# A Mamba block with an FP4 feed-forward: state carries, norm statistics and evictions go to ScalarE, the residual add to the feed-forward's head

## The chip, the cores and the metric

One core of a Trainium2 chip runs the whole program. The metric is the device time of one execution in microseconds (us), the median of the runs shown. The engines are TensorE (PE; its weight loads are shown as PEld), VectorE (DVE), ScalarE (ACT), GpSimd (POOL) and SyncE (SP), which issues all DMAs of this kernel. Each engine runs its instructions in the order in which they were written; semaphores make one wait for another.

## The reference

The input x has 8192 rows of 512 numbers. A layernorm with a scale and a shift from a modulation vector, a Mamba mixer, a gated residual, a second layernorm, a feed-forward with FP4-quantized operands, and a second gated residual:

```python
h = _layernorm(x) * (1 + ca) + sa
x = x + ga * mamba(h)
h = _layernorm(x) * (1 + cb) + sb
x = x + gb * ffn(h)

# mamba(h): 1024 inner channels (DI), 16 states (NS), delta rank 32
xc, z = split(h @ W_in.T)
xc = silu(causal_conv4(xc))                 # 4 taps, per channel
dlt, B, C = split(xc @ W_xproj.T)
delta = softplus(dlt @ W_dt.T + b_dt)
s = exp(delta * A) * s + delta * B * xc     # a scan over the 8192 rows
y = sum_n(s * C) + xc * D
out = (y * silu(z)) @ W_out.T
# ffn(h): silu(q(h) @ q(w_gate).T) * (q(h) @ q(w_up).T), quantized again, @ q(w_down).T
```

Everything is computed in fp32.

## The kernel before, in words

**Three stages.** A prologue (about 155 us) quantizes the gate and up weights and prepares the first chunk. The scan part runs to about 4310 us. The feed-forward part takes the rest, 64 tiles of 128 rows.

**The scan part** cuts the 8192 rows into 16 chunks `k` of 512 rows (T). In a chunk the 1024 channels are 8 blocks `d` of 128 partitions, worked through in four pairs `h`; the 16 states in 8 groups `g` of two. One *slot* is one channel block with two states: 64 slots a chunk, 1024 in all, in the order k, h, g, i (i is the block within the pair). `unit(slot)` is the heart of it:

- two scans on VectorE (L454), each over 512 rows of one state: `da` (exp of delta times A, made by ScalarE into PSUM, L434) times the running state plus `db` (delta times x times B, made by GpSimd two slots ahead, L425, three buffers);
- the carry: the last column of the two scans is copied into `state`, where the same block finds it 64 slots later;
- the product with C, and its transposes into the accumulator `y` in PSUM on TensorE (`add_up`, L368).

There are two kinds of slots. A *far* slot (odd i, and g % 4 not 3: 24 of the 64) scans into an SBUF tile `hp`; its carry is a ScalarE copy (L462) and its product is made by GpSimd (L471). A *near* slot (40 of the 64) scans into the one PSUM tile `hs`; its carry is a VectorE copy (L474) and its product `hc` is made by VectorE (L476). ScalarE's order within a slot is: the first exp of the next slot, the carry (far slots), the second exp of the next slot, then the slot's side work. The PSUM holds two `da` tiles, so an exp waits until the scan of the same number one slot earlier is through.

**The side work** is put into slots by hand: `at(slot, moment, fn, ...)` files a function for a slot, and `run` calls it. The moments are BEGIN (before the scans are issued), GAP (after the scans and exps, before the next `db` and the product) and END (after the product). A table of offsets in the loop over `k` (from `for k in range(NC)` on) says which step goes where. The steps that the change touches:

- `norm`, `norm_x`, `norm_t`, `norm_out`: the layernorm of the next chunk's rows. Statistics on VectorE (bn_stats, L217 to L221), the power -1/2 on GpSimd (L223), the offset on VectorE (L230), the normalized rows on ScalarE (L232), transposes on TensorE, scale and shift on ScalarE (L247).
- `conv_mm`, `conv_raw`, `conv_diag`, `conv_taps`, `conv_act`, `conv_out`: the four-tap convolution as matmuls. `raw` holds three columns from the chunk before (`tail`) and 512 new ones. GpSimd copies the three columns in (L274) and the new tail out (L276); the second copy reads what ScalarE wrote into `raw` (L275). `conv_diag` makes the four diagonal tap matrices on ScalarE (L268).
- `prep_mm`, `prep`: delta with a softplus on ScalarE, with a table load before and after it (L327, L434). `make_du`: delta times x on GpSimd (L334), one for each block of the pair.
- `z_mm`, `z_act`, `z_out`: the z half of in_proj, its tanh on ScalarE (L353) and the silu on VectorE (L357).
- `skip_act`, `skip`: x times D into `y`. `gate` (L379): y times silu(z) on VectorE, two halves, after the pair's last slot. `gate_t`, `gate_out` (L390): transposes back.
- `out_mm`, `out_add`: out_proj, and the residual add on VectorE (L403): the rows of x are loaded again (`load_x` with key "r"), the product is added from PSUM, and the sum is stored to the DRAM tiles `x1`.

PSUM is full: one bank (`mm`) serves z, out_proj, gate_t, x_proj and half of prep_mm in turn; another (`cv`) serves the convolution, the norm's transposes and the other half.

**The feed-forward part** is put in order by a scheduler, not by hand. For each tile of 128 rows, `normed` loads the rows from `x1`, takes the layernorm (`_layernorm`, bn_stats on VectorE and the power on GpSimd), applies scale and shift on GpSimd (L808, L809) and quantizes; `up` and `down` are the matmuls with the quantization between them. `head` prepares a tile ahead.

## Time and profile before

| | us |
|---|---|
| median of 3 runs (6424.08 to 6426.37) | 6424.61 |
| profiled execution | 6427.96 |
| its span, first to last instruction | 6426.2 |
| prologue | about 155 |
| scan part, to the last scan | about 155 to 4304 |
| feed-forward part, one tile in its steady state | 31.4 |

| engine | busy us | share |
|---|---|---|
| PE | 5533.2 | 86% |
| DVE | 5079.5 | 79% |
| POOL | 4033.9 | 63% |
| ACT | 2858.3 | 44% |

The shares are means over stages with different limits, so they are read stage by stage. In the groups by line, a row gives line, engine, operation, output and inputs with their shapes, the number of instructions, their busy time in us and the mean ns of one, and then the idle time of the engine just before them with what ended it. In the timeline, a row gives start and duration in us and, in brackets, the idle time before it and who ended it. Neighbouring instructions of an engine can overlap by about 0.1 us, so what an instruction costs is read from the starts.

### The profile page before, as it was taken

The numbers are of one execution on the slowest core, as the hardware profiler recorded it, in microseconds if no ns is written. First come the engines' busy times: TensorE is split into PE (matmuls) and PEld (weight loads), VectorE is DVE, ScalarE is ACT, GpSimd is POOL, SyncE is SP. The second block draws the span as 40 slices with busy tenths as digits, with TensorE's granted clock in tenths as the row PEclk, the third lists the DMA queues.
The fourth block names the chain that finished last, engine by engine and source line by source line (L and its number), as shares of the span: only waits on it lengthen the run. The fifth ranks groups of instructions, "written<-read, shape, count | busy, mean of one in ns | idle before, by whom it ended". The sixth has DMA issues, their size and how long they took to land.

```text
span 6426.2 us, 60794 instructions
## 1 busy us (share of the span) xinstructions
PE 5533.2 (86%) x20772; PEld 3284.8 (51%) x20772; DVE 5079.5 (79%) x5711; ACT 2858.3 (44%) x4940; POOL 4033.9 (63%) x2222
## 2 busy tenths in 40 slices
PE   7788878888888888887888888767999999999999
PEld 4455555555555555555555555543444444444444
DVE  7988888888888888888888888988566666666564
ACT  5555555555555555555555555532222222222222
POOL 5888888888888888888888888872222222222221
PEclk9899888889888898988988889778999999999999
DMA  5444444444444444444444444440000000000000
GB/s 186 135 145 139 138 140 140 144 140 144 143 136 140 143 142 144 136 145 135 143 141 142 144 140 140 152 162 23 22 17 17 17 17 17 18 18 17 17 17 12
DMA packets 220557, 659.83 MB, mean 103 GB/s; under 512 B 24371, under 2 KB 36787, under 8 KB 220246
## 3 DMA queue, kind: packets, MB, share of 16 engines
q1 hardware_dynamic: 220246, 655.94, 31.4%
q8 instruction: 163, 2.67, 0.2%
q14 instruction: 148, 1.21, 0.1%
HBM read 615.48 MB, written 40.38 MB: 102 GB/s over the span
## 4 chain that ended last, share of the span: by engine, by line
PE 53%; DVE 30%; POOL 6%; ACT 5%; issue 5%; DMA 1%; DVEq 0%; SPq 0%; POOLq 0%; ACTq 0%
DVE hs L454 13%; PE pg L874 9%; PE po L891 9%; PE pu L874 9%; DVE hp L454 7%; PE po L396 6%; PE y L368 6%; DVE hc L476 5%; PE cv L254 5%; PE cv L282 4%; POOL db L425 4%; PE pz L344 2%; POOL hp L471 2%; PE pt L842 1%; DVE z L379 1%
## 5 line engine op out<-in xcount | busy, mean ns | idle before, releaser
L425 POOL TENSOR_TENSOR db<-bc,du 128x1024 f32<-128x1024 f32 x1024 | 2396.0, 2358 | 17.4 <-DVE hs L454 13.2
L434 ACT ACTIVATE da<-delta,na 128x512 f32<-128x512 f32 x2048 | 1394.3, 686 | 1548.5 <-DVE hs L454 969.5
L454 DVE TENSOR_TENSOR_SCAN hs<-da,state,db 128x512 f32<-128x512 f32 x1280 | 1647.4, 1287 | 230.6 <-POOL db L425 122.1
L368 PE MATMUL y<-ident,hc 128*128 128x128 f32 x5120 | 783.4, 303 | 457.5 <-DVE hc L476 456.9
L87 POOL TENSOR_TENSOR hq<-xn,sc 128x1408 f32<-128x1408 f32 x64 | 189.1, 2955 | 1466.3 <-DVE xn L82 1466.3
L471 POOL TENSOR_TENSOR hp<-hp,bc 128x1024 f32<-128x1024 f32 x384 | 905.4, 2358 | 186.1 <-ACT state L462 184.9
L454 DVE TENSOR_TENSOR_SCAN hp<-da,state,db 128x512 f32<-128x512 f32 x768 | 941.6, 1268 | 60.8 <-ACT da L434 54.6
L368 PEld LDWEIGHTS y<-ident,hc 128*128 128x128 f32 x5120 | 652.0, 156 | 656.4 <-DVE hc L476 570.7
L476 DVE TENSOR_TENSOR hc<-hs,bc 128x1024 f32<-128x1024 f32 x640 | 779.9, 1219 | 0.3 <-issue 0.3
L874 PE MATMUL pg<-wg,xqT 128*128 128x512 f32 (+1 forms) x1536 | 651.8, 568 | 44.0 <-ACT xqT L866 44.0
L254 PE MATMUL cv<-hT,w_in 128*128 128x512 f32 x1024 | 560.4, 698 | 128.5 <-ACT delta L327 103.3
L874 PE MATMUL pu<-wu,xqT 128*128 128x512 f32 (+1 forms) x1536 | 635.9, 557 | 0.0
L891 PE MATMUL po<-wd,hqT 128*128 128x512 f32 x1408 | 616.2, 593 | 0.0
L880 DVE TENSOR_TENSOR h<-g,pu 128x512 f32<-128x512 f32 (+1 forms) x192 | 122.9, 640 | 541.9 <-PE pu L874 528.4
L879 ACT ACTIVATE g<-pg 128x512 f32<-128x512 f32 (+1 forms) x192 | 107.7, 561 | 957.7 <-PE pg L874 957.7
L282 PE MATMUL cv<-raw,taps 128*128 128x512 f32 x1024 | 510.7, 645 | 5.9 <-POOL raw L274 4.9
L344 PE MATMUL pz<-w_in,hT 128*128 128x256 f32 x2048 | 490.7, 395 | 1.4 <-DVE z L357 1.4
L874 PEld LDWEIGHTS pg<-wg,xqT 128*128 128x128 f32 x1536 | 290.1, 192 | 361.2 <-issue 250.3
L396 PE MATMUL po<-w_o,xc 128*128 128x512 f32 x1024 | 466.7, 599 | 3.3 <-DVE xr L403 2.5
L874 PEld LDWEIGHTS pu<-wu,xqT 128*128 128x128 f32 x1536 | 291.8, 190 | 312.7 <-issue 243.5
L368 PE MATMUL y<-ident,hp 128*128 128x128 f32 x3072 | 436.5, 289 | 0.0
L368 PEld LDWEIGHTS y<-ident,hp 128*128 128x128 f32 x3072 | 389.8, 151 | 88.0 <-issue 72.4
(112 smaller groups left out, 6274.0 us busy)
## 6 DMA issues: line engine op xcount, KB each, us to landing
bc<-bc SPq DMA_DIRECT2D x1024, 512.0 KB, 4.7
xn<-in_x_dram SPq DMA_DIRECT2D x64, 256.0 KB, 4.8
xr<-in_x_dram SPq DMA_DIRECT2D x64, 256.0 KB, 4.9
x<-xr SPq DMA_DIRECT2D x64, 256.0 KB, 2.1
x<-x SPq DMA_DIRECT2D x64, 256.0 KB, 2.6
out_dram<-x SPq DMA_DIRECT2D x64, 256.0 KB, 2.0
w_in<-in_w_inT_dram SPq DMA_DIRECT2D x2, 2048.0 KB, 10.1
wm<-in_wmod_dram SPq DMA_DIRECT2D x8, 512.0 KB, 4.8
```

The costliest lines, as they stand in the source:

```text
L254: nc.tensor.matmul(ps, lhsT=w_in[:, f, o : o + P], rhs=hT[k][:, f, :], start=(f == 0), stop=(f == NK - 1),)
L282: nc.tensor.matmul(v, lhsT=taps[:, i, :], rhs=raw[:, i : i + T], start=(i == 0), stop=(i == 3))
L344: nc.tensor.matmul(pz[:, b, :], lhsT=hT[k][:, f, t0 : t0 + P], rhs=w_in[:, f, o : o + DH * P], start=(b == 0 and f == 0), stop=(f == NK - ...
L368: nc.tensor.matmul(y[:, j, i * P : (i + 1) * P], lhsT=src[:, j * P : (j + 1) * P], rhs=ident, start=start and j % 2 == 0, stop=stop, is_tr ...
L396: nc.tensor.matmul(pend["po", k, j], lhsT=xcs[k, d][:, j * P : (j + 1) * P], rhs=w_o[:, d, :], start=(d == 0), stop=(d == ND - 1),)
L425: nc.gpsimd.tensor_tensor(db, bct[slot // DH, 0], dus[k, h, i].unsqueeze(1).to_broadcast([P, GN, T]), ALU.mult)
L434: nc.scalar.activation(da, deltas[k, h][:, i, :], AF.Exp, scale=na[:, d, n : n + 1])
L454: nc.vector.tensor_tensor_scan(to[:, q, :], pend.pop(("da", slot, q)), db[:, q, :], state[:, d, n : n + 1], ALU.mult, ALU.add,)
L471: nc.gpsimd.tensor_tensor(to, to, c_rows, ALU.mult)
L476: nc.vector.tensor_tensor(hc, hs, c_rows, ALU.mult)
L874: nc.tensor.matmul(ps[:, :w], lhsT=qT[:, k, :], rhs=wt[:, k, o : o + w], start=(k == 0), stop=(k == NK - 1),)
L891: nc.tensor.matmul(po, lhsT=hT[:, f, :], rhs=wd[:, f, :], start=(f == 0), stop=(f == NF - 1))
```

## The change

State carry: all slots copy the carry on ScalarE; the VectorE copy of near slots is gone.

Norm: the statistics are taken on ScalarE. `norm_sum` copies the rows onto themselves with a running sum and scales the sum to the negative mean; `norm_var`, a slot later, squares the centred rows with a running sum and adds eps; `norm_rstd` is the power on GpSimd, at the next slot's BEGIN; `norm_x` makes the offset and the normalized rows on ScalarE.

Row tails: ScalarE copies the three columns into `raw`, and the new tail from PSUM.

out_proj: `out_keep` copies the product from PSUM into an SBUF tile on ScalarE, at GAP where `out_add` was at END, and stores it to the DRAM tiles `mo`. x isn't loaded a second time here. The feed-forward's head loads both `mo` and x and adds them on GpSimd.

Moved steps: the gate's two halves from GAP and END of the first slot after the pair to its END and the next slot's GAP; `gate_t`, `gate_out`, `skip_act` and `skip` one slot later; the first product's transposes of a pair one slot later; the second block's delta-x product to the slot before the pair begins; some of z's and out_proj's slots by one.

```diff
-        def norm(k, j):
+        def norm_sum(k, j):
             xt = xts["n", k, j]
-            st = small.tile([P, 6], F32, tag="st", name="st")
-            nc.vector.bn_stats(st, xt)
-            mv = small.tile([P, 2], F32, tag="mv", name="mv")
-            nc.vector.bn_aggr(mv, st)
+            su = small.tile([P, 1], F32, tag="su", name="su")
+            nc.scalar.activation(xt, xt, AF.Copy, accum_out=su)
+            nm = small.tile([P, 1], F32, tag="nm", name="nm")
+            nc.scalar.activation(nm, su, AF.Copy, scale=-1.0 / DM)
+            pend["nm", k, j] = nm
+
+        def norm_var(k, j):
+            xt, nm = xts["n", k, j], pend["nm", k, j]
+            xh = s1.tile([P, DM], F32, tag="xh", name=f"xh_{k}_{j}")
+            ss = small.tile([P, 1], F32, tag="ss", name="ss")
+            nc.scalar.activation(xh, xt, AF.Square, bias=nm, accum_out=ss)
             ve = small.tile([P, 1], F32, tag="ve", name="ve")
-            nc.vector.tensor_scalar(ve, mv[:, 1:2], EPS, None, ALU.add)
+            nc.scalar.activation(ve, ss, AF.Identity, bias=eps, scale=1.0 / DM)
...
+        def norm_rstd(k, j):
             rstd = small.tile([P, 1], F32, tag="rstd", name="rstd")
-            nc.gpsimd.tensor_tensor(rstd, ve, mhalf, ALU.pow)
+            nc.gpsimd.tensor_tensor(rstd, pend.pop(("ve", k, j)), mhalf, ALU.pow)
...
         def norm_x(k, j):
             off = small.tile([P, 1], F32, tag="off", name="off")
-            nc.vector.tensor_scalar(off, mv[:, 0:1], rstd, -1.0, ALU.mult, ALU.mult)
-            nc.scalar.activation(xh, xt, AF.Identity, bias=off, scale=rstd)
+            nc.scalar.activation(off, nm, AF.Copy, scale=rstd)
+            nc.scalar.activation(
+                pend["xh", k, j], xts.pop(("n", k, j)), AF.Identity, bias=off, scale=rstd
+            )
...
         def conv_raw(k, d):
-            nc.gpsimd.tensor_copy(raw[:, 0:3], tail[:, d, :])
             nc.scalar.activation(raw[:, 3 : T + 3], v, AF.Copy)
-            nc.gpsimd.tensor_copy(tail[:, d, :], raw[:, T : T + 3])
+            nc.scalar.activation(raw[:, 0:3], tail[:, d, :], AF.Copy)
+            nc.scalar.activation(tail[:, d, :], v[:, T - 3 : T], AF.Copy)
...
-        def out_add(k, j):
-            xt = xts.pop(("r", k, j))
-            nc.vector.tensor_tensor(xt, xt, pend.pop(("po", k, j)), ALU.add)
-            nc.sync.dma_start(x1[k][j * P : (j + 1) * P, :], xt)
+        def out_keep(k, j):
+            po = xp.tile([P, DM], F32, tag="x", name=f"po_{k}_{j}")
+            nc.scalar.activation(po, pend.pop(("po", k, j)), AF.Copy)
+            nc.sync.dma_start(mo[k][j * P : (j + 1) * P, :], po)
...
             carry = state[:, d, g * GN : (g + 1) * GN]
-            if far:
-                nc.scalar.activation(carry, to[:, :, T - 1], AF.Copy)
+            nc.scalar.activation(carry, to[:, :, T - 1], AF.Copy)
...
             else:
-                nc.vector.tensor_copy(carry, hs[:, :, T - 1])
                 hc = pools["h"].tile([P, GN, T], F32, tag="hc", name=f"hc_{slot}")
                 nc.vector.tensor_tensor(hc, hs, c_rows, ALU.mult)
                 if g == 0 and i == 0:
-                    at(slot + 1, BEGIN, add_up, slot, hc)
+                    at(slot + 2, BEGIN, add_up, slot, hc)
...
-            for m, o in enumerate((-3, -1, 15, 21, 37, 43, 45, 47)):
+            for m, o in enumerate((-3, -1, 15, 22, 38, 42, 44, 46)):
...
-                at(b + o - 3, GAP, norm, k, j)
-                at(b + o - 2, GAP, norm_x, k, j)
+                at(b + o - 3, GAP, norm_sum, k, j)
+                at(b + o - 2, GAP, norm_var, k, j)
+                at(b + o - 1, BEGIN, norm_rstd, k, j)
+                at(b + o - 1, GAP, norm_x, k, j)
...
                 for i in range(DH):
-                    at(e + o + 2 + i, GAP, make_du, k, h, i)
-                    at(r + 2 + 4 * i, GAP, skip_act, k, h * DH + i)
-                    at(r + 4 + 4 * i, BEGIN, skip, k, h * DH + i)
+                    at((r - 1 if r else -2) if i else e + o + 2, GAP, make_du, k, h, i)
+                    at(r + 3 + 4 * i, GAP, skip_act, k, h * DH + i)
+                    at(r + 5 + 4 * i, BEGIN, skip, k, h * DH + i)
                 r += SLOT_S
                 for j in range(0, NJ, 2):
-                    at(r, END if j else GAP, gate, k, h, j)
+                    at(r + (1 if j else 0), GAP if j else END, gate, k, h, j)
                 for i in range(DH):
-                    at(r + 1 + 2 * i, BEGIN, gate_t, k, h, i)
-                    at(r + 2 + 2 * i, GAP, gate_out, k, h, i)
-            for j, o in enumerate((5, 8, 23, 29)):
-                at(n + (o - 3 if k < NC - 1 or j == NJ - 1 else j - 4), BEGIN, load_x, k, j, "r")
+                    at(r + 2 + 2 * i, BEGIN, gate_t, k, h, i)
+                    at(r + 3 + 2 * i, GAP, gate_out, k, h, i)
+            for j, o in enumerate((6, 9, 23, 29)):
                 at(n + o, BEGIN, out_mm, k, j, 0)
                 at(n + o + 1, BEGIN, out_mm, k, j, 1)
-                at(n + o + 2, END, out_add, k, j)
+                at(n + o + 2, GAP, out_keep, k, j)
...
             xt = io.tile([P, DM], F32, tag="x1", name=f"x1_{t}")
-            nc.sync.dma_start(xt, x1[t // NJ][t % NJ * P : (t % NJ + 1) * P, :])
+            nc.sync.dma_start(xt, mo[t // NJ][t % NJ * P : (t % NJ + 1) * P, :])
             h2 = work.tile([P, DM], F32, tag="h2", name=f"h2_{t}")
+            nc.sync.dma_start(h2, x[t * P : (t + 1) * P, :])
+            nc.gpsimd.tensor_tensor(xt, xt, h2, ALU.add)
             _layernorm(nc, small, xt, h2, mhalf)
```

In the slots of a chunk (0 to 63) ScalarE's side work then stands so, where it changes: slots 1, 29, 49 raw, tails and taps; 21 gate_out and the same; 35 gate_out, x times D and the same; 43 z's tanh and the same; 45 z's tanh; 51 gate_out, x times D and a norm_sum; 53 gate_out, norm_x and a norm_sum; 57 norm_out and a norm_sum; 59 softplus, norm_x and a norm_sum; 61 norm_out and norm_x. All of these are far slots.

## The prediction

> **What bounds the kernel now.** First the busy shares by stretch (columns: stretch, its length, busy us of PE, PEld, DVE, ACT and POOL, granted clock, DMA share, GB/s): one millisecond of the scan part, and the feed-forward part.
>
> ```profile
> 3000.00:4000.00 1000.00, 832.36 (x3586) 540.54 (x3585) 880.44 (x956) 552.33 (x999) 834.09 (x444) 0.89 0.43 141
> 4600.00:6426.00 1826.00, 1763.53 (x4921) 860.01 (x4919) 1096.48 (x1355) 444.46 (x633) 398.03 (x279) 1.00 0.05 17
> ```
>
> In the scan part (1024 slots, about 155 to 4310 us) VectorE is busiest at 88%, GpSimd and TensorE have 83%, ScalarE 55%. In the feed-forward part TensorE is busy 97% and nothing else can matter. So I ask what VectorE does and waits for in a scan slot: the groups by line, then the waits.
>
> ```profile
> L454 DVE TENSOR_TENSOR_SCAN hs<-da,state,db 128x512 f32<-128x512 f32 x1280 | 1647.4, 1287 | 230.6 <-POOL db L425 122.1 <-ACT da L434 25.3 <-DVE hs L454 1.4
> L474 DVE COPY state<-hs 128x2 f32<-128x2 f32 x640 | 100.8, 157 | 16.7
> L462 ACT ACTIVATE state<-hp 128x2 f32<-128x2 f32 x384 | 78.5, 204 | 178.4 <-DVE hp L454 178.4
> L403 DVE TENSOR_TENSOR xr<-xr,po 128x512 f32<-128x512 f32 x64 | 43.7, 684 | 67.8 <-PE po L396 67.8
> ```
> ```profile
> POOL tail L276 <- ACT raw L275: 403.9, 125, 7.2
> DVE hs L454 <- POOL db L425: 122.1, 87, 2.2
> DVE z L379 <- PE y L368: 68.3, 38, 2.8
> DVE xr L403 <- PE po L396: 67.8, 41, 12.9
> DVE hp L454 <- ACT da L434: 54.6, 47, 1.6
> ```
>
> (Waits: total us, times, longest.) GpSimd stands 404 us before a three-column copy, and VectorE 122 us for the products GpSimd then makes late. Last the timeline, for how tight a slot is:
>
> ```profile
> 2035.00 2.45 DVE L454 TENSOR_TENSOR_SCAN hp<-da,state,db 128x512 f32<-128x512 f32 x2
> 2037.36 2.66 DVE L454 TENSOR_TENSOR_SCAN hs<-da,state,db 128x512 f32<-128x512 f32 x2
> 2040.06 0.16 DVE L474 COPY state<-hs 128x2 f32<-128x2 f32 x1
> 2040.14 1.22 DVE L476 TENSOR_TENSOR hc<-hs,bc 128x1024 f32<-128x1024 f32 x1
> 2042.94 2.69 DVE L454 TENSOR_TENSOR_SCAN hs<-da,state,db 128x512 f32<-128x512 f32 x2 [1.58 <-ACT da L434]
> ```
> ```profile
> 2037.48 0.20 ACT L462 ACTIVATE state<-hp 128x2 f32<-128x2 f32 x1 [0.48 <-DVE hp L454]
> 2037.59 0.68 ACT L434 ACTIVATE da<-delta,na 128x512 f32<-128x512 f32 x1
> 2038.29 1.28 ACT L327 ACT_TABLE_LOAD   x1
> 2039.58 1.26 ACT L327 ACTIVATE delta<-pd,bdt 128x512 f32<-128x512 f32 x2
> 2040.86 1.28 ACT L434 ACT_TABLE_LOAD   x1
> 2042.16 1.30 ACT L434 ACTIVATE da<-delta,na 128x512 f32<-128x512 f32 x2
> ```
>
> A near slot (scans into PSUM, product hc on VectorE) lasts 2.70 + 0.08 + 1.13 = 3.91 us, a far slot (product on GpSimd) 2.37 us. A chunk has 24 far and 40 near slots: 213 us, plus 16 near-near seams of 0.22, 24 gate, z and convolution operations of 0.6, four norms, four residual adds, and some 23 us of waits: about 262; the trace repeats every 261 to 262 us.
>
> **The change, part by part.** Per run: 16 chunks, 15 of them with the next chunk's convolution and norm.
>
> *Leaves VectorE.* Norm statistics: 43.0 + 11.6 + 9.8 + 12.2 = 77 us in four groups of 64, some 60 without the overlap of neighbours. The residual add: 39 us (43.7 less overlap) and 48 of its 67.8 us of waits (the other 20 fall after the last scan, where TensorE works anyway). ScalarE takes its place in waiting for out_proj, and exp waits behind it: 0.5 us each, which fits the slack below, unless TensorE is late. Gate a step later: the 68 us for y go, since y's last transposes then have a slot of 4 us more; the first transposes of the next y wait for slot 2 instead, behind nothing that VectorE needs. Row tails: GpSimd loses 256 copies (56 us) and the 404 us of waiting; of VectorE's 122 us for db I take 116, because GpSimd's work per chunk (64 + 24 products of 2.34, eight of 1.27, four pow) is 218 of 261 us. The moved delta-x product stands just ahead of the db that needs it, in a slot without a far product; it adds nothing. Sum: 60 + 87 + 68 + 116 = 331 us gained.
>
> *The near carry.* At first sight 640 copies of 0.16 go; they cost 0.08 us each in the timeline. But in the built program every one of the 640 hc products now waits for ScalarE's carry of its own slot, where before none waited for ScalarE. Hops in this trace: scan's end to ScalarE's carry 0.033, the carry 0.205, ScalarE to VectorE 0.033 (z after its tanh). So hc starts 0.271 us after the scan, not 0.111: 0.16 worse, 640 times, less 5 us at slots with other VectorE work in between: 98 us lost. Ends: 51 us gained if it cost nothing, 131 lost with the 0.077 hop that GpSimd shows.
> [...]
>
> *What stands ahead of that carry.* hc now needs ScalarE to have finished the previous slot's side work and one exp. After a far slot's last scan, at T, ScalarE is free at T + 0.84; with side work W and an exp of 0.61 it reaches the carry at T + 1.45 + W, and the scan is done at T + 2.60: VectorE stalls W - 1.15, less 0.6 for each VectorE operation of that slot. Before, it could hide 2.3 (softplus with table loads, W = 3.87: stall 1.58, as shown). After near slots about 2.3 to 2.9 stay hidden. Work by effective time: raw, row start, tail and taps 0.50 + 0.11 + 0.11 + 1.17 = 1.89; gate_out 0.48; dx 0.61; norm_out 1.37. Not in the trace: Copy with a sum, between 0.58 (L275) and 0.80 (L232), and its 128x1 follower between 0.11 and 0.29: I take 0.70 together, nearest to the plain copy; Square between 0.58 and 0.80 lies in near slots and is hidden; off and x-hat 1.0 together. Far slots of a chunk, stall each: three softplus 2.72; softplus with x-hat and sum (slot 59) 4.42; two z tanh that VectorE now awaits without an hc before it (43, 45) 1.5 each; slot 35 1.83, 21 and 61 1.22 each, 57 0.92, 29 0.74, 51 0.64, 53 0.43, 1 and 49 0.14 each. Sum 22.9 us, against 5.0 (da, 79.9 us over 16) and 1.8 (z) now: 16.1 more in 15 chunks, 4.4 in the last: 246 us lost.
>
> *Feed-forward.* Per tile one load more on SP, landing in 2.6 us, and one GpSimd add of 1.29 (as L808), queued behind xq's 1.06. bn_stats then starts some 2.6 us later; VectorE now waits 4.07 us for pu after the first product, so TensorE's 31.4 us per tile stay. Without that spare, each us would cost 64. At the start of this part VectorE no longer waits for out_proj (L403, 12.9 and 7.2 us) before the first statistics, but the head waits for its loads and the add: 5 us gained, up to as much lost among the four w_down quantizations. Prologue: eight norms on ScalarE beside a half-busy VectorE; within 2 us.
>
> *Sum.* 98 + 246 = 344 lost, 331 + 5 = 336 gained. Stalls overlap a little (my before-chunk of 262 stands against 260.8 measured, so I take 5% off the losses): 327 against 336, 9 us gained. The profiled run took 6428.0 (span 6426.2 and 1.8 around it), 3.4 above the median of 6424.6; against the median: 6416.
>
> **Rivals.** *ScalarE's side work stays hidden*, faster: if slots 1, 21, 29, 35, 49, 51, 53, 57 and 61 find VectorE late anyway, 7.3 us x 15 = 109 go: about 6307. For it: ScalarE has 45% idle. Against: the exp wait after softplus follows my rule to 0.1 us.
> *ScalarE's waits for TensorE pass on*, slower: tanh (104 us), raw (33) and now out_proj (68) are waited for on ScalarE in order, with the carry and hence hc behind. It decides where such a wait brings W past 1.15 us (far) or 2.3 (near); half of 205 us gives 6519. For it: TensorE is 83% busy and late at out_proj 41 times. Against: out_mm starts a slot later in half the cases.
> *It does nothing for GpSimd*, since db then waits for buffers (three) and scans: the 116 shrink to 30 and 6500 follows. Against: GpSimd's longest waits sit right before the late db.
>
> **How the numbers follow.** Forecast (the sides cancel, 6380 to 6455): 0.45. Faster rival 0.28; the two slower ones together 0.27. The range leaves out the outer ends: 6320 to 6510. A difference under 0.2% (13 us) cannot be told from none; of the forecast's 0.45 about 0.19 lie below 6412, 0.15 within, 0.11 above 6437: faster 0.47, same 0.15, slower 0.38.
>
> **What would show it.** After: no wait of POOL on raw; db waits under 20 us; no wait of z for y; hc with 640 idles of about 0.27 us released by ScalarE's carry (some 170 us and the far-slot stalls beside them, 250 to 400 us together); VectorE's scans waiting less for da, since hc waits first; the feed-forward tile still 31.4 us. I am wrong if hc starts as soon as the scan ends, if hc's idle is far above 400 us, or if the tile's 31.4 us changes.

## The result and the profile after

The changed kernel takes 6601.6 us (median of 4 runs, 6601.2 to 6602.2) against 6424.4 before (4 runs): 1.0275 of the time before, 95% interval 1.0257 to 1.0293. That is 177 us slower where 6416 was forecast, and outside the range.

The time is all in the scan part. From the first scan to the end of the last one it takes 4322.6 us (155.96 to 4478.55) where it took 4146.9 (157.17 to 4304.06); what follows takes 2120.9 us against 2122.1, and a feed-forward tile still 31.40. From chunk to chunk (mean of 14 chunks) the trace repeats every 272.76 us, where it was 261.67.

Groups by line of the changed kernel (busy us, mean ns | idle of the engine before them, and what ended it). Of the tile names, xc is the convolution's result, y the accumulator, dx is x times D; po, pz and pgt are out_proj's product, z's product and the gate's transposes, which take turns in the `mm` bank:

```profile
L468 DVE TENSOR_TENSOR_SCAN hs<-da,state,db 128x512 f32<-128x512 f32 x1280 | 1646.4, 1286 | 83.7 <-DVE hc L488 1.4 <-POOL db L439 1.2 <-DVE hs L468 0.9
L488 DVE TENSOR_TENSOR hc<-hs,bc 128x1024 f32<-128x1024 f32 x640 | 783.4, 1224 | 518.7 <-ACT state L475 483.1 <-PE y L382 34.9 <-PE pt L255 0.3
L306 DVE SCALAR_TENSOR_TENSOR xc<-raw,cv 128x512 f32<-128x512 f32 x128 | 86.2, 673 | 88.3 <-ACT raw L301 88.3
L371 DVE SCALAR_TENSOR_TENSOR z<-z,pz 128x512 f32<-128x512 f32 x128 | 87.3, 682 | 71.4 <-ACT z L367 71.4
L393 DVE TENSOR_TENSOR z<-z,y 128x512 f32<-128x512 f32 x128 | 85.8, 671 | 10.5 <-PE y L382 10.5
```

The waits that the change was to remove are gone: db 1.2 us (122 before), da none, z for y 10.5 (68), no residual add. In their place hc, which waited for nothing before, stands idle for 518.7 us. Beside it xc waits 88.3 us, where it waited 16. The waits of the changed kernel that belong to this second row (total us, times, longest):

```profile
ACT raw L301 <- PE cv L296: 197.8, 74, 7.0
PE po L410 <- DVE z L371: 55.9, 15, 4.1
DVE hp L468 <- PE y L382: 36.5, 29, 2.0
DVE hc L488 <- PE y L382: 34.9, 14, 2.5
```

The tanh of the convolution waits for TensorE up to 7.0 us at a time, and once in each of 15 chunks out_proj's product (po) waits for z, a wait that the trace before does not have. VectorE's timeline of the changed kernel shows both kinds (start, length, and in brackets the idle time before it and what ended it):

```profile
2042.54 1.22 DVE L488 TENSOR_TENSOR hc<-hs,bc 128x1024 f32<-128x1024 f32 x1 [4.82 <-ACT state L475]
2054.69 1.23 DVE L488 TENSOR_TENSOR hc<-hs,bc 128x1024 f32<-128x1024 f32 x1 [0.24 <-ACT state L475]
2115.91 1.22 DVE L488 TENSOR_TENSOR hc<-hs,bc 128x1024 f32<-128x1024 f32 x1 [2.95 <-ACT state L475]
2164.19 0.69 DVE L306 SCALAR_TENSOR_TENSOR xc<-raw,cv 128x512 f32<-128x512 f32 x1 [4.57 <-ACT raw L301]
2170.04 1.22 DVE L488 TENSOR_TENSOR hc<-hs,bc 128x1024 f32<-128x1024 f32 x1 [2.52 <-PE y L382]
2248.44 1.23 DVE L488 TENSOR_TENSOR hc<-hs,bc 128x1024 f32<-128x1024 f32 x1 [2.35 <-ACT state L475]
```

The plain wait for the carry is 0.24 us. The 4.82 stands behind slot 59 (softplus with x-hat and a sum), the 2.95 behind a softplus, and these were forecast. The 4.57 at slot 25, the 2.52 at slot 26 and the 2.35 at slot 44 were not.

Counting the scans in the timeline puts each wait to its slot. Means over 14 chunks, in us; "forecast" is the prediction's stall of the slot ahead, to which the plain 0.24 is to be added for hc; "without the moves" is experiment 14 below, which has the carry, the norm, the tails and out_proj's eviction on ScalarE, but the old slots of the gate and z:

| wait of VectorE | forecast | after | without the moves (E14) |
|---|---|---|---|
| hc at 14, 28, 42 (softplus in 13, 27, 41) | 2.72 | 2.94, 2.94, 2.94 | 2.95, 2.92, 2.94 |
| hc at 60 (slot 59) | 4.42 | 4.69 | 4.69 |
| hc at 22, 36 | 1.22, 1.83 | 1.40, 2.01 | 0.92, 0.89 |
| hc at 52, 54 | 0.64, 0.43 | 0.84, 0.70 | under 0.3 |
| hc at 58, 62 | 0.92, 1.22 | 1.13, 1.31 | 1.14, 1.31 |
| z at 43 and 45 | 1.5, 1.5 | 1.73, 1.37 | none |
| hc at 44 | none | 2.35 | 0.92 |
| xc at 25, then hc at 26 for y | none | 4.53, 2.49 | none |
| hp's scan at 5 for y | none | 1.88 | 2.14 |
| xc at 11 | none new (1.07 before) | 1.48 | none |

### The profile page after: what moved, and what is told of

The parts are those of the page before. It is cut to its first block, busy times and chain, and to the rows that moved or that the text cites. A ratio compares the mean times of both kernels' runs of the same rounds, so it can differ in the third digit from the quotient of the medians.

```text
span 6599.4 us, 61356 instructions
## 1 busy us (share of the span) xinstructions
PE 5577.0 (85%) x20772; PEld 3297.9 (50%) x20772; DVE 4924.5 (75%) x4751; ACT 3079.8 (47%) x6348; POOL 4087.5 (62%) x2031
## 4 chain that ended last, share of the span: by engine, by line
PE 51%; DVE 29%; ACT 14%; issue 4%; POOL 1%; DMA 1%; DVEq 0%; SPq 0%; POOLq 0%; ACTq 0%
DVE hp L468 9%; PE pg L891 9%; DVE hs L468 9%; PE po L908 9%; PE pu L891 9%; PE po L410 7%; DVE hc L488 7%; PE cv L296 6%; PE y L382 5%; ACT da L448 3%; PE cv L268 3%; PE pz L358 2%; PE pt L859 1%; ACT taps L282 1%; ACT state L475 1%
## 5 line engine op out<-in xcount | busy, mean ns | idle before, releaser
L488 DVE TENSOR_TENSOR hc<-hs,bc 128x1024 f32<-128x1024 f32 x640 | 783.4, 1224 | 518.7 <-ACT state L475 483.1
L382 PE MATMUL y<-ident,hc 128*128 128x128 f32 x5120 | 768.5, 301 | 357.9 <-DVE hc L488 357.1
L358 PE MATMUL pz<-w_in,hT 128*128 128x256 f32 x2048 | 527.3, 416 | 73.2 <-ACT delta L341 65.8
L268 PE MATMUL cv<-hT,w_in 128*128 128x512 f32 x1024 | 519.0, 654 | 73.5 <-ACT delta L341 72.0
L410 PE MATMUL po<-w_o,xc 128*128 128x512 f32 x1024 | 511.8, 648 | 77.3 <-DVE z L371 55.9
L296 PE MATMUL cv<-raw,taps 128*128 128x512 f32 x1024 | 532.5, 668 | 6.9 <-ACT taps L282 6.9
L358 PEld LDWEIGHTS pz<-w_in,hT 128*128 128x128 f32 x2048 | 423.7, 213 | 146.4 <-ACT delta L341 69.9
```

The costliest lines, as they stand in the source:

```text
L268: nc.tensor.matmul(ps, lhsT=w_in[:, f, o : o + P], rhs=hT[k][:, f, :], start=(f == 0), stop=(f == NK - 1),)
L296: nc.tensor.matmul(v, lhsT=taps[:, i, :], rhs=raw[:, i : i + T], start=(i == 0), stop=(i == 3))
L358: nc.tensor.matmul(pz[:, b, :], lhsT=hT[k][:, f, t0 : t0 + P], rhs=w_in[:, f, o : o + DH * P], start=(b == 0 and f == 0), stop=(f == NK - ...
L382: nc.tensor.matmul(y[:, j, i * P : (i + 1) * P], lhsT=src[:, j * P : (j + 1) * P], rhs=ident, start=start and j % 2 == 0, stop=stop, is_tr ...
L410: nc.tensor.matmul(pend["po", k, j], lhsT=xcs[k, d][:, j * P : (j + 1) * P], rhs=w_o[:, d, :], start=(d == 0), stop=(d == ND - 1),)
L488: nc.vector.tensor_tensor(hc, hs, c_rows, ALU.mult)
```

## The experiments

All are timed beside the kernel before, 4 runs or more each; that kernel's median was between 6425.7 and 6427.5 in the four sets. "E" stands for the labels below.

| | kernel | us | ratio to before, 95% interval |
|---|---|---|---|
| E1 | after, near carry on VectorE | 6321.4 | 0.9838 (0.9824 to 0.9853) |
| E2 | after, z in its old slots | 6515.8 | 1.0141 (1.0124 to 1.0157) |
| E3 | before, near carry on ScalarE | 6495.9 | 1.0108 (1.0093 to 1.0123) |
| E4 | before, tails on ScalarE | 6385.0 | 0.9938 (0.9923 to 0.9952) |
| E5 | after, norm on VectorE | 6505.9 | 1.0124 (1.0109 to 1.0139) |
| E6 | after, gate in its old slots | 6522.7 | 1.0150 (1.0134 to 1.0165) |
| E7 | before, out_keep and x added in the head | 6388.0 | 0.9941 (0.9925 to 0.9958) |
| E8 | after, carry on VectorE, z old | 6348.7 | 0.9879 (0.9864 to 0.9894) |
| E9 | after, only z's m = 3 old | 6508.5 | 1.0127 (1.0110 to 1.0144) |
| E10 | before, gate a step later | 6496.0 | 1.0111 (1.0096 to 1.0126) |
| E11 | before, norm on ScalarE | 6399.5 | 0.9960 (0.9945 to 0.9974) |
| E12 | after, carry on VectorE, gate old | 6358.2 | 0.9895 (0.9881 to 0.9910) |
| E13 | after, carry on VectorE, gate and z old | 6292.1 | 0.9789 (0.9773 to 0.9806) |
| E14 | E13 with the carry on ScalarE | 6414.1 | 0.9978 (0.9969 to 0.9988) |
| E15 | a version from E1 | 6270.2 | 0.9758 (0.9743 to 0.9772) |

### The near carry: E1 and E3

E1 is the changed kernel with

```diff
-            nc.scalar.activation(carry, to[:, :, T - 1], AF.Copy)
+            if far:
+                nc.scalar.activation(carry, to[:, :, T - 1], AF.Copy)
...
             else:
+                nc.vector.tensor_copy(carry, hs[:, :, T - 1])
```

> The changed kernel with one part undone: VectorE itself copies the carry of a near slot, as before the change. Theory (the loss is the wait of hc for ScalarE's carry and for the side work ahead of it): hc's 483 us of waits for the carry go, 51 us of copies come back (640 x 0.08), and behind softplus and the like VectorE waits for da instead, 1.6 us where it waited 2.7; some 8 of the 21 us of stalls per chunk stay. Gain 16 x (6.4 + 13), about 300: 6300 us (6250 to 6380). Rival (TensorE, 85% busy, is what runs late, and VectorE only waits for ScalarE because ScalarE waits for TensorE): the waits move from hc to xc, hp and z, and less than 100 us is gained: above 6500.

Measured: 6321.4, 280 us below the changed kernel and 104 below the kernel before. Groups of E1:

```profile
L468 DVE TENSOR_TENSOR_SCAN hs<-da,state,db 128x512 f32<-128x512 f32 x1280 | 1646.9, 1287 | 111.1 <-ACT da L448 25.4 <-POOL db L439 1.0 <-DVE hs L468 0.9
L490 DVE TENSOR_TENSOR hc<-hs,bc 128x1024 f32<-128x1024 f32 x640 | 780.8, 1220 | 1.1 <-issue 1.1
L306 DVE SCALAR_TENSOR_TENSOR xc<-raw,cv 128x512 f32<-128x512 f32 x128 | 86.1, 673 | 57.1 <-ACT raw L301 57.1
```

hc's idle falls from 518.7 to 1.1 us, and xc's from 88.3 to 57.1 without any step of the convolution having been touched. So the rest of the change is a gain of 104 us as long as VectorE copies the carry itself, and this one copy's engine turns it into the loss of 177. The theory's number holds, and TensorE is not what bounds the changed kernel by itself.

E3 is the kernel before with the reverse edit.

```diff
-            if far:
-                nc.scalar.activation(carry, to[:, :, T - 1], AF.Copy)
+            nc.scalar.activation(carry, to[:, :, T - 1], AF.Copy)
...
-                nc.vector.tensor_copy(carry, hs[:, :, T - 1])
```

> The kernel before with one part of the change alone: ScalarE copies every carry, VectorE none. Theory: hc starts 0.16 us later 640 times (98 us), and side work on ScalarE beyond 1.15 us in a far slot stalls hc: about 17 us a chunk without the norm sums and tails, where the waits for da and z were 6.8; 150 us more. Some of the 122 us of waits for db vanish behind it. 6580 to 6670, hc idle 350 to 500 us. Rival (side work stays hidden, only the hop counts): at most 98 us, 6525 or less. Rival (one VectorE copy less is a gain): below 6425.

Measured: 6495.9, a loss of 70 only, less than the theory and less than the bare hop was priced at; the first rival's number, but not its reason. The stalls themselves are there (2.94, 2.95 and 2.94 us at 14, 28 and 42), and hc idles 19.4 us a chunk, some 310 in all. But the other waits of VectorE shrink from 23.9 to 13.1 us a chunk: da 5.0 to 0, z for y 4.5 to 2.7, db 8.0 to 6.1, the residual add 3.4 to 2.2, z 1.9 to 0.8. A stall ahead of a wait takes the wait's place. So the same carry costs 70 us in one kernel and 280 in the other.

### The parts that leave VectorE and GpSimd: E4, E7, E11, E5

E4, the kernel before with the tails on ScalarE:

```diff
-            nc.gpsimd.tensor_copy(raw[:, 0:3], tail[:, d, :])
             nc.scalar.activation(raw[:, 3 : T + 3], v, AF.Copy)
-            nc.gpsimd.tensor_copy(tail[:, d, :], raw[:, T : T + 3])
+            nc.scalar.activation(raw[:, 0:3], tail[:, d, :], AF.Copy)
+            nc.scalar.activation(tail[:, d, :], v[:, T - 3 : T], AF.Copy)
```

> The kernel before with one part of the change alone: the convolution's row start and tail copied by ScalarE, not GpSimd. Theory: GpSimd's 404 us of waits for raw and 56 us of copies go, VectorE's 122 us of waits for db fall to under 10: about 116 us gained, less some 10 for 0.22 us more ScalarE work ahead of da: 6310 to 6330. Rival (db is late for want of buffers and scans): 30 us gained, 6390.

Measured: 41 us gained, as little as the rival said, but not for its reason. Groups of E4:

```profile
L454 DVE TENSOR_TENSOR_SCAN hs<-da,state,db 128x512 f32<-128x512 f32 x1280 | 1646.6, 1286 | 141.9 <-POOL db L425 33.1 <-ACT da L434 25.4 <-DVE hs L454 1.4
L454 DVE TENSOR_TENSOR_SCAN hp<-da,state,db 128x512 f32<-128x512 f32 x768 | 941.3, 1267 | 87.4 <-ACT da L434 54.7 <-PE y L368 22.7 <-POOL db L425 5.5
L223 POOL TENSOR_TENSOR rstd<-ve,mhalf 128x1 f32<-128x1 f32 x64 | 38.6, 604 | 98.7 <-DVE ve L221 81.1 <-DMA bc<-bc 17.6
```

89 of the 122 us of waits for db went. 1.85 us a chunk stay, at slot 62: GpSimd now stands before the norm's power until VectorE has the variance (81 us, 37 before). And hp's scan at slot 5 waits for TensorE's transposes (22.7 us, 1.2 before), z for its tanh 57 us (38), z for y 79 (68): TensorE was late next.

E7, the kernel before with out_proj evicted by ScalarE and x added in the feed-forward head:

```diff
-            xt = xts.pop(("r", k, j))
-            nc.vector.tensor_tensor(xt, xt, pend.pop(("po", k, j)), ALU.add)
-            nc.sync.dma_start(x1[k][j * P : (j + 1) * P, :], xt)
+            po = xp.tile([P, DM], F32, tag="x", name=f"po_{k}_{j}")
+            nc.scalar.activation(po, pend.pop(("po", k, j)), AF.Copy)
+            nc.sync.dma_start(mo[k][j * P : (j + 1) * P, :], po)
...
+            nc.sync.dma_start(h2, x[t * P : (t + 1) * P, :])
+            nc.gpsimd.tensor_tensor(xt, xt, h2, ALU.add)
```

> The kernel before with one part of the change alone: out_proj evicted by ScalarE, x added in the feed-forward head, no second load of x in the scan part. Theory of the prediction: VectorE loses 39 us of adds and 48 us of waits: 87 us gained, 6338 (6330 to 6360), and ScalarE's waits for out_proj lie inside the 2.3 us that a copy of VectorE's own leaves hidden. Rival (ScalarE's wait for TensorE passes on to da): only the 39 us and little more, 6380 or above, with da waits of VectorE well above 80 us. The feed-forward part unchanged within 5 us.

Measured: 39 us gained, the 39 us of adds and nothing of their 48 us of waits. But da is not later (5.0 us a chunk as before): the wait did not pass on through ScalarE as the rival had it. xc at slot 11 waits 2.88 us instead of 1.07, z at 44 2.08 instead of 1.52, db 8.9 a chunk instead of 8.0: VectorE, arriving earlier, finds TensorE and GpSimd where they were.

E11, the kernel before with the norm statistics on ScalarE (the changed kernel's four norm functions and their slots; in short):

```diff
-                at(b + o - 3, GAP, norm, k, j)
-                at(b + o - 2, GAP, norm_x, k, j)
+                at(b + o - 3, GAP, norm_sum, k, j)
+                at(b + o - 2, GAP, norm_var, k, j)
+                at(b + o - 1, BEGIN, norm_rstd, k, j)
+                at(b + o - 1, GAP, norm_x, k, j)
```

> The kernel before with one part of the change alone: the norm statistics on ScalarE. Theory of the prediction: 60 us of VectorE time gained, 6365. Theory now: 4.8 us a chunk of VectorE work and 1.85 us of db at slot 62 go; softplus with x-hat and a sum in slot 59 makes da 3.3 us late at slot 61 and z 1 us at slot 62: net some 2.6 us a chunk, 6385 (6370 to 6425).

Measured: 26 us gained where the prediction had 60. da at slot 61 is 3.30 us late (0.31 before) and z at 62 1.03, as the softplus of slot 59 has x-hat and a sum beside it.

E5, the changed kernel with the norm back on VectorE:

```diff
-                at(b + o - 3, GAP, norm_sum, k, j)
-                at(b + o - 2, GAP, norm_var, k, j)
-                at(b + o - 1, BEGIN, norm_rstd, k, j)
-                at(b + o - 1, GAP, norm_x, k, j)
+                at(b + o - 3, GAP, norm, k, j)
+                at(b + o - 2, GAP, norm_x, k, j)
```

> The changed kernel with one part undone: the norm statistics back on VectorE, and x-hat a slot earlier. Theory (each part on ScalarE stalls hc by what it adds ahead of the near carry): some 60 us of VectorE work come back; the stalls of hc at slots 58, 60 and 62 of a chunk (1.13, 4.69, 1.31 in the changed kernel) fall to about 0.3, 1.7 and 0.6, 4.5 us a chunk or 68 us; and as with the tails alone on ScalarE, one db a chunk is late behind the power on GpSimd, up to 28 us. Sum about +20: 6620 (6590 to 6640), so moving the norm gave next to nothing. Rival (the norm on ScalarE is a main part of the loss): 6550 or less. Rival (the norm's move is worth its 60 us of VectorE time): 6660.

Measured: 6505.9, 96 us below the changed kernel, which is the first rival's size and not the theory's. hc's waits fall by 6.8 us a chunk (4.69 to 1.67 at 60, as expected; those at 52 to 58 and 62 to under 0.3), for 4.1 us of VectorE work put back. But another 2.85 us a chunk, 43 us over 15 chunks, fell where no step was touched: xc at slot 25 waits 1.68 us instead of 4.53. The next part shows that TensorE's clock is behind this.

### Slot 23: E2, E9 and TensorE's clock

E2, the changed kernel with

```diff
-            for m, o in enumerate((-3, -1, 15, 22, 38, 42, 44, 46)):
+            for m, o in enumerate((-3, -1, 15, 21, 37, 43, 45, 47)):
```

> The changed kernel with one part undone: z's matrix products back to their old slots (m = 3 to 7 at 21, 37, 43, 45, 47). Theory (z in slot 23 holds the one accumulator that out_proj's product at the start of slot 23 needs, so conv taps, tanh, xc and hc come late): the waits of xc at slot 25 (4.5 us a chunk, before the change 0) and of hc for y at slot 26 (2.5) go, the stall of hc at slot 44 (2.35, raw and taps behind z's tanh in slot 43) becomes a shorter one; 6 to 8 us a chunk, 90 to 120 us: 6480 to 6510. TensorE's wait for z ahead of out_proj falls from 56 us to nearly nothing. Rival (tanh is late because ScalarE is): within 20 us of the changed kernel, xc still waits 4 us at slot 25.

Measured: 86 us gained, just short of the 90 to 120 expected. The wait of po for z is gone, xc at 25 and hc at 26 cost 0.4 us together, and hc at 44 0.9. A new wait of 4.08 us for z's tanh at slot 38 takes part of it back. E9 changes one of the numbers only:

```diff
-            for m, o in enumerate((-3, -1, 15, 22, 38, 42, 44, 46)):
+            for m, o in enumerate((-3, -1, 15, 21, 38, 42, 44, 46)):
```

> The changed kernel with one number undone: z's fourth product (m = 3) from slot 22 back to 21, the others stay. Theory: in the changed kernel TensorE idles 3.75 us in slot 23 until z leaves the accumulator, and the out_proj product after it then takes 6.78 us at half clock instead of 3.60; both go: xc at slot 25 waits 1 to 1.8 us instead of 4.5, hc at 26 next to nothing instead of 2.5; z at slot 22 waits 0.6. 4.5 to 5.5 us a chunk: 6520 to 6535, and the product after it takes 3.60 us with no wait ahead of it. Rival (the 86 us that all old z slots gave came from slots 37 to 47): within 25 us of the changed kernel.

Measured: 93 us gained by one slot number, somewhat more than expected. TensorE's timeline from slot 22 on, first in the changed kernel, then in E5, then in E9 (lengths of the groups, and in brackets the idle time):

```profile
2148.46 1.09 PE L382 MATMUL y<-ident,hc 128*128 128x128 f32 x8 [0.15 <-DVE hc L488]
2153.31 6.78 PE L410 MATMUL po<-w_o,xc 128*128 128x512 f32 x8 [3.75 <-DVE z L371]
2159.92 3.60 PE L296 MATMUL cv<-raw,taps 128*128 128x512 f32 x8
```
```profile
2106.47 1.04 PE L371 MATMUL y<-ident,hc 128*128 128x128 f32 x8
2110.76 3.70 PE L399 MATMUL po<-w_o,xc 128*128 128x512 f32 x8 [3.26 <-DVE z L360]
2114.30 3.60 PE L285 MATMUL cv<-raw,taps 128*128 128x512 f32 x8
```
```profile
2109.57 1.04 PE L382 MATMUL y<-ident,hc 128*128 128x128 f32 x8
2110.44 3.60 PE L410 MATMUL po<-w_o,xc 128*128 128x512 f32 x8
2113.88 3.60 PE L296 MATMUL cv<-raw,taps 128*128 128x512 f32 x8
```

z's product was moved to slot 22, so z leaves the one `mm` bank at the end of slot 23, and out_proj's product, filed for the beginning of slot 23, needs that bank. TensorE stands 3.75 us. Then the same eight matmuls take 6.78 us instead of 3.60: the clock fell while it stood, 0.6 us before the wait's end. In E5 the wait is 3.26 us, and the matmuls take 3.70. The stretches from the start of slot 23, and from the end of the wait, first of the changed kernel, then of E5 (the last three columns are the granted clock, the DMA share and GB/s):

```profile
2148.50:2153.30 4.80, 1.06 (x8) 0.82 (x8) 4.45 (x5) 2.57 (x5) 3.97 (x2) 0.94 0.36 133
2153.30:2160.10 6.80, 6.79 (x9) 2.91 (x10) 6.04 (x5) 1.45 (x3) 2.73 (x2) 0.54 0.23 77
```
```profile
2105.96:2110.76 4.80, 1.54 (x12) 1.18 (x10) 4.45 (x5) 2.57 (x5) 4.00 (x2) 1.00 0.36 122
2110.76:2117.56 6.80, 6.79 (x16) 3.09 (x17) 6.03 (x5) 1.45 (x3) 2.75 (x2) 1.00 0.20 77
```

The granted clock is 0.54 against 1.00; in the same 6.8 us TensorE does 9 matmuls against 16. The convolution's taps queue behind, its tanh is late on ScalarE by up to 7.0 us, and xc, the y transposes and hc follow. The wait at this place and the length of the eight matmuls in chunks 1 to 14 of the trace:

| kernel | wait, us | the eight matmuls, us |
|---|---|---|
| after | 3.75 to 4.10 | 6.49 to 6.78 |
| E6 | 3.75 to 4.11 | 5.36 to 6.55 |
| E12 | 3.69 to 4.04 | 5.11 to 6.72 |
| E5 | 3.25 to 3.27 (one 3.76) | 3.70 (the one: 6.23) |
| E1 | 1.75 to 2.62 (two of 2.76) | 3.70 (the two: 5.22 and 5.15) |
| E2, E9 | none | 3.60 |

So the wait of 3.75 us costs twice: once as idle time, and 3 us more in the matmuls after it. In E5, where the steps of the norm (slots 51 to 61) were undone, it is the second cost that is gone at slot 25. The wait's length is not what decides that, as two chunks of E15 (the last experiment) show, with the same wait of 2.76 us in both. Under each are the busy time of TensorE, the granted clock, the DMA share and GB/s in the steps of the 3.41 us grid on which the clock changes in the traces:

```profile
2010.97 5.15 PE L410 MATMUL po<-w_o,xc 128*128 128x512 f32 x8 [2.76 <-DVE z L371]
2007.10:2010.51 3.41, 1.11 (x10) 1.00 0.68 223
2010.51:2013.93 3.42, 2.96 (x4) 0.50 0.43 153
```
```profile
2263.91 3.70 PE L410 MATMUL po<-w_o,xc 128*128 128x512 f32 x8 [2.76 <-DVE z L371]
2259.68:2263.10 3.42, 1.47 (x11) 1.00 0.75 247
2263.10:2266.51 3.41, 2.60 (x6) 1.00 0.46 154
```

Where the wait lies on the steps decides here. In the first chunk 2.30 us of it fall into one step, and the next step has half the clock; in the second, 1.95 us. In the 13 fast chunks of E5 a step's end cuts the wait in two, and no step has more than 1.68 us idle; in its chunk 15 a wait of only 3.08 lies almost whole in one step, and the matmuls take 5.40. How the norm's steps come to shift the wait on this grid is not shown.

### The gate a step later: E6, E10, E8, E12

E6, the changed kernel with the gate's steps back:

```diff
-                    at(slot + 2, BEGIN, add_up, slot, hc)
+                    at(slot + 1, BEGIN, add_up, slot, hc)
...
-                    at(r + 3 + 4 * i, GAP, skip_act, k, h * DH + i)
-                    at(r + 5 + 4 * i, BEGIN, skip, k, h * DH + i)
+                    at(r + 2 + 4 * i, GAP, skip_act, k, h * DH + i)
+                    at(r + 4 + 4 * i, BEGIN, skip, k, h * DH + i)
...
-                    at(r + (1 if j else 0), GAP if j else END, gate, k, h, j)
+                    at(r, END if j else GAP, gate, k, h, j)
...
-                    at(r + 2 + 2 * i, BEGIN, gate_t, k, h, i)
-                    at(r + 3 + 2 * i, GAP, gate_out, k, h, i)
+                    at(r + 1 + 2 * i, BEGIN, gate_t, k, h, i)
+                    at(r + 2 + 2 * i, GAP, gate_out, k, h, i)
```

> The changed kernel with one part undone: gate, its transposes, gate_out, delta-x skips and the first transposes of y a slot earlier, as before the change (out_proj stays). Theory (a step later put dx and gate_out into far slots, where only 1.15 us of ScalarE work is hidden, and the first y transposes behind conv taps): the stalls of hc at 12, 22, 30, 36, 52 and 54 fall by 0.4 to 1.4 us each, some 4.5 us a chunk; hp's scan no longer waits 1.9 and 0.6 for y at slots 5 and 53; z waits for y again, 2.7 to 4.5 us a chunk where it waited 0.6. Net 3 us a chunk, 50 us gained: 6550 (6520 to 6580). Rival (the step later is a gain of the 58 us that z's waits for y lost): 6650 to 6670.

Measured: 79 us gained, at the edge of the theory's range. hc at 22 falls to 0.91, at 36 to 0.92, at 44 to 1.22, at 52 and 54 below 0.3. z for y costs 1.0 us a chunk instead of 0.6, not the 3 and more that were expected: hc is late anyway, and y is ready. So putting the gate back costs nothing there. (hc at 2 and 50 rises from 0.32 to 0.91: the gate's second half, 0.66 us of VectorE work in slots 1 and 49, no longer covers that much of the stall.)

E10, the kernel before with the gate a step later (the same lines the other way, and out_proj's first two products from slots 5 and 8 to 6 and 9):

```diff
-                    at(r + 2 + 4 * i, GAP, skip_act, k, h * DH + i)
-                    at(r + 4 + 4 * i, BEGIN, skip, k, h * DH + i)
+                    at(r + 3 + 4 * i, GAP, skip_act, k, h * DH + i)
+                    at(r + 5 + 4 * i, BEGIN, skip, k, h * DH + i)
...
-                at(r, END if j else GAP, gate, k, h, j)
+                at(r + (1 if j else 0), GAP if j else END, gate, k, h, j)
...
-            for j, o in enumerate((5, 8, 23, 29)):
+            for j, o in enumerate((6, 9, 23, 29)):
```

> The kernel before with one part of the change alone: gate, its transposes, gate_out, skips and the first transposes of y a slot later. Theory of the prediction: the 68 us of z's waits for y go and nothing comes instead: 6357. Theory now: z waits 0.6 instead of 4.5 us a chunk, but hp's scan waits for y at slots 5 and 53, 1.5 to 3 us a chunk, and TensorE late elsewhere takes some more: 15 to 45 us gained, 6380 to 6410.

Measured: 70 us lost, where the prediction had 68 gained. Waits of E10:

```profile
DVE z L357 <- ACT z L353: 98.8, 49, 9.7
DVE xr L403 <- PE po L396: 87.8, 43, 12.3
DVE xc L292 <- ACT raw L287: 30.1, 30, 1.3
DVE z L379 <- PE y L368: 20.6, 16, 1.4
PE pz L344 <- ACT xc L390: 65.2, 19, 3.9
```

48 of the 68 us for y do go (20.6 left), and z's tanh takes 60 more (38 before), the residual add 20 more, xc 14. The last row is new: z's product waits for gate_out. TensorE's timeline of E10 at slot 37:

```profile
2160.31 1.09 PE L368 MATMUL y<-ident,hc 128*128 128x128 f32 x8 [1.92 <-DVE hc L476]
2165.28 6.18 PE L344 MATMUL pz<-w_in,hT 128*128 128x256 f32 x16 [3.88 <-ACT xc L390]
```

The gate's transposes and z's product share the `mm` bank. gate_out, a slot later now, frees it in slots 21 and 37, where z's product stands at the beginning. At slot 37 TensorE waits 3.88 us, and the product then takes 6.18 us (granted clock 0.59 over it), where at full clock it takes 3.62. At slot 21 it begins when gate_out ends, later than before, but in 13 of 14 chunks without idle time of TensorE, and takes 3.72 or less. z is 1.87 us late at slot 22 and 2.09 at 38, where it was 0.33 and under 0.3.

E8 and E12 have the carry on VectorE, and each one of the two moves undone (E12's edit in short; it puts back all that E6 does):

```diff
+                nc.vector.tensor_copy(carry, hs[:, :, T - 1])
...
-            for m, o in enumerate((-3, -1, 15, 22, 38, 42, 44, 46)):
+            for m, o in enumerate((-3, -1, 15, 21, 37, 43, 45, 47)):
```

> The changed kernel with two parts undone: near carry on VectorE and z's products in their old slots. Theory: the two losses are mostly apart; of the 86 us that the old z slots gave alone, the xc wait at slot 25 (1.8 us a chunk left with the carry on VectorE) and some of the z waits at 43 and 45 go: 20 to 50 us below the kernel with the carry alone, 6270 to 6300. Rival (with hc free of ScalarE the old slots of z give nothing): 6315 to 6330.

```diff
+                nc.vector.tensor_copy(carry, hs[:, :, T - 1])
...
-                at(r + (1 if j else 0), GAP if j else END, gate, k, h, j)
+                at(r, END if j else GAP, gate, k, h, j)
...
-                at(r + 3 + 2 * i, GAP, gate_out, k, h, i)
+                at(r + 2 + 2 * i, GAP, gate_out, k, h, i)
```

> The changed kernel with two parts undone: near carry on VectorE, and the gate's steps in their old slots. Theory (with the carry on VectorE dx and gate_out are hidden in far slots too, so the old slots give only the y waits back and take hp's away): z waits for y 3 us a chunk more, hp's scan at 5 and 53 one to three less: 6310 to 6350. Rival (the 79 us that the old slots gave in the changed kernel add to those of the carry): 6240 to 6270.

Measured: 6348.7 and 6358.2, both slower than E1 (6321.4), by 27 and 37 us; E8 lies above both its expectations, E12 just above the theory's. TensorE's timeline of E8, at slot 37:

```profile
2089.18 1.09 PE L382 MATMUL y<-ident,hc 128*128 128x128 f32 x8 [1.75 <-DVE hc L490]
2093.60 6.62 PE L358 MATMUL pz<-w_in,hT 128*128 128x256 f32 x16 [3.33 <-ACT xc L404]
```

As in E10, with the gate moved and z not, z's product waits for gate_out and takes 6.62 us (granted clock 0.55), and VectorE's z is 4.74 us late at slot 38. In E12, with z moved and the gate not, it is slot 23 that is slow (the table above), and xc at 25 waits 3.73 us where E1 has 1.81. So the two moves belong together: beside this carry, each without the other costs more than both.

### What the carry costs beside what: E13 and E14

E13 undoes the carry, z's slots and all of the gate's slots (its edit in short); the norm, the tails, out_keep and the add in the head stay, and with them the delta-x product's new slot and out_proj's first two, 6 and 9, neither of which was tested by itself.

```diff
+                nc.vector.tensor_copy(carry, hs[:, :, T - 1])
...
-            for m, o in enumerate((-3, -1, 15, 22, 38, 42, 44, 46)):
+            for m, o in enumerate((-3, -1, 15, 21, 37, 43, 45, 47)):
...
-                at(r + (1 if j else 0), GAP if j else END, gate, k, h, j)
+                at(r, END if j else GAP, gate, k, h, j)
```

> The changed kernel with three parts undone (near carry on VectorE, z and the gate's steps in their old slots): what stays is the norm, the tails and out_proj's eviction on ScalarE and x added in the feed-forward head. Theory (these three, worth 41, 39 and 26 us alone, are apart from each other): 6319 (6300 to 6340), as much as the changed kernel with only the carry undone, so that the moves together are worth nothing. Rival (ScalarE's work adds up until da is late more often): 6350 to 6400.

E14 is E13 with the carry as in the changed kernel:

```diff
-            if far:
-                nc.scalar.activation(carry, to[:, :, T - 1], AF.Copy)
+            nc.scalar.activation(carry, to[:, :, T - 1], AF.Copy)
...
-                nc.vector.tensor_copy(carry, hs[:, :, T - 1])
```

> The kernel of e13 with the near carry on ScalarE and nothing else changed. Theory (the carry's price grows with ScalarE's added work alone: stalls of hc at 52 to 62 as in the changed kernel, 4.7 at 60): 130 to 200 us above e13, about 6480. Rival (the price is the 70 us of the carry alone, and the moves made the rest): about 6390.

Measured: 6292.1 and 6414.1. E13 is below the range that was expected. The three parts together, with those two new slots, gain 135 us (26, 41 and 39 alone, 106 in sum); what the two slots add is not shown. The carry beside them costs 122, a little under the theory's 130 to 200 and well above the 70 it costs alone. Groups of E13, then of E14:

```profile
L490 DVE TENSOR_TENSOR hc<-hs,bc 128x1024 f32<-128x1024 f32 x640 | 780.2, 1219 | 1.1 <-issue 0.8 <-PE cv L296 0.3
L371 DVE SCALAR_TENSOR_TENSOR z<-z,pz 128x512 f32<-128x512 f32 x128 | 87.6, 684 | 78.0 <-ACT z L367 78.0
L393 DVE TENSOR_TENSOR z<-z,y 128x512 f32<-128x512 f32 x128 | 87.1, 681 | 72.0 <-PE y L382 72.0
```
```profile
L488 DVE TENSOR_TENSOR hc<-hs,bc 128x1024 f32<-128x1024 f32 x640 | 783.0, 1223 | 424.8 <-ACT state L475 424.5 <-PE y L382 0.2
L371 DVE SCALAR_TENSOR_TENSOR z<-z,pz 128x512 f32<-128x512 f32 x128 | 87.0, 680 | 27.1 <-ACT z L367 27.1
L393 DVE TENSOR_TENSOR z<-z,y 128x512 f32<-128x512 f32 x128 | 86.9, 680 | 26.2 <-PE y L382 26.2
```

hc idles 424 us more, but the copies' 51 us, da's 8.0 us a chunk and 97 us of waits of z are gone in exchange. With E2, E6, E8 and E12 every combination of the carry and the two moves has been timed (us):

| slots of gate and z | carry on VectorE | carry on ScalarE | the carry's price |
|---|---|---|---|
| both old | 6292.1 (E13) | 6414.1 (E14) | 122 |
| gate moved | 6348.7 (E8) | 6515.8 (E2) | 167 |
| z moved | 6358.2 (E12) | 6522.7 (E6) | 165 |
| both moved | 6321.4 (E1) | 6601.6 (after) | 280 |

The moves cost 29 us beside a carry on VectorE and 187 beside one on ScalarE. What the 187 are is read slot by slot between E14 and the changed kernel (13.3 us a chunk): xc at 25 and hc at 26, 7.0 us; z 3.0 more; hc's waits for the carry 3.7 more (slots 22, 36, 44, 52, 54, where dx, gate_out or z's tanh were put in far slots); xc at 11, 1.5; less 2.0 that y waits are shorter. That is 13.2.

### A version: E15

The changed kernel with the carry on VectorE, z's last three products and two x-hats in other slots:

```diff
+                nc.vector.tensor_copy(carry, hs[:, :, T - 1])
...
-            for m, o in enumerate((-3, -1, 15, 22, 38, 42, 44, 46)):
+            for m, o in enumerate((-3, -1, 15, 22, 38, 43, 45, 47)):
...
-                at(b + o - 3, GAP, norm_sum, k, j)
-                at(b + o - 2, GAP, norm_var, k, j)
-                at(b + o - 1, BEGIN, norm_rstd, k, j)
-                at(b + o - 1, GAP, norm_x, k, j)
-                at(b + o, BEGIN, norm_t, k, j)
+                s, q = (1 if k > 1 and j == 3 else 0), (1 if k > 1 and j > 1 else 0)
+                at(b + o - 3 + s, GAP, norm_sum, k, j)
+                at(b + o - 2 + s, GAP, norm_var, k, j)
+                at(b + o - 1 + q, BEGIN, norm_rstd, k, j)
+                at(b + o - 1 + q, GAP, norm_x, k, j)
+                at(b + o, END if q else BEGIN, norm_t, k, j)
```

> A version: the changed kernel with the near carry on VectorE, z's products m = 5 to 7 in their old slots 43, 45, 47, and the third and fourth x-hat of a chunk a slot later (60 and 62, near slots) with the fourth sum out of the softplus slot 59. Theory: of e1's waits da at 61 falls from 3.3 to 1.6, z at 62 goes, z at 43 and 45 (3.1) becomes 1.4 at 44, da at 45 goes: 4 to 6 us a chunk, 6230 to 6260. Rival (TensorE is late next, and takes it): above 6290.

Measured: 6270.2, faster than both kernels (0.9758 of the time before) and 51 us below E1, a little less than expected. da at 61 is 1.56 us late instead of 3.31, z at 43 and 45 (3.1) became 1.42 at 44; z at 62 went from 1.01 to 1.52, xc at 25 from 1.81 to 2.46, and da at 62 is new with 0.61. E13 with the x-hats moved in the same way was not tried.

## Why the prediction was wrong

The prediction took 336 us of gains against 327 of losses. By E1 the gains were 104 and the losses 280. (Taken apart in another order they differ: the carry put first, by E3, costs 70.)

**The near carry: right in mechanism.** It said that hc would wait for ScalarE's carry of its own slot; 593 of 640 show it. The plain wait is 0.24 us after the scan where 0.27 was said (0.11 would have been free): ScalarE's copy out of PSUM takes 0.17 us, and 0.205 had been taken from the copies out of SBUF. Why the built program puts the carry's and the product's reads of hs in order is not shown by any run; what the trace shows is the wait.

**"What stands ahead of that carry": right slot by slot.** The rule W - 1.15 gave 2.72 behind a softplus, and 2.70 came (2.94 less 0.24); 4.42 behind slot 59, and 4.45 came; 1.83 and 1.77 at 35; 1.22 and 1.16 at 21. The one wrong item is slot 43: its z wait of 1.5 came (1.73), but raw, tails and taps are queued behind the tanh there, and hc at 44 stalls 2.1 more, 32 us in 15 chunks, which had been taken as nothing. As a price, 98 + 246 less 5% was too high (and the 5% came from a chunk of 260.8 us, where the trace has 261.67): 280 in the changed kernel, 122 without the moves, 70 in the kernel before. The waits for da and z were taken off, the waits for y, out_proj and db that a late hc also swallows were not.

**The failed step is "Sum: 60 + 87 + 68 + 116 = 331 us gained".** Its terms alone measured 26 (norm), 39 (residual add), minus 70 (gate) and 41 (db). What VectorE no longer executes was gained: its busy time falls from 230.9 to 224.8 us a chunk, by 6.1, and the period of E1 is 7.3 shorter. Of what it no longer waits for, only the other 1.2 were gained. The waits of VectorE in a chunk, in us, over 0.2 each:

| ended by | before | E1 | E13 |
|---|---|---|---|
| db | 8.0 | 0 | 0.3 |
| y, for z | 4.5 | 1.1 | 4.8 |
| out_proj | 3.4 | 0 | 0 |
| da | 5.0 | 10.8 | 8.0 |
| z's tanh | 1.9 | 4.1 | 4.5 |
| xc's tanh | 1.1 | 3.8 | 0 |
| y's transposes, for hp's scan | 0 | 3.0 | 3.7 |
| sum | 23.9 | 22.8 | 21.3 |

In E1 14.8 us of waits (the first three rows) were removed, and 13.7 came in the next four. The prediction asked only of two removed waits what would come in their place. For out_proj's it named exp on ScalarE and took it as hidden; E7 agrees (da 5.0 a chunk as before), yet xc, z and db waited longer. For y its answer, transposes "behind nothing that VectorE needs", is wrong: hp's scan waits for TensorE's transposes at slot 5, and gate_out holds z's bank.

**A step that was priced only half: z's products moved.** The text priced z's new slots by ScalarE's work at 43 and 45, and did not place m = 3 against out_proj's product on the one bank. By E9 that is 93 us in the changed kernel.

**The rivals.** The slower rival about ScalarE's waits for TensorE happened in a narrow form: tanh's wait rose from 104 to 198 us and passed on to xc and hc, 93 us by E9 where half of 205 was its price; but it came from z's move and the clock, not from those waits as they stood. The rival about GpSimd had the size (86 less; 75 less in E4) and not the reason. They were held apart, one instead of the other; both came. The faster rival is wrong: the stalls at 21, 29, 35 and 61 are there.

**The signs.** No wait of GpSimd for raw, db under 20 us, z for y nearly gone, the tile's 31.4 us: as said. hc's idle was to be 250 to 400 us and anything far above was to mean error; it was 519. The feed-forward start gained about 1 us, not 5.
